# More sorted pairs, fewer own columns, and half of the sort comparisons on VectorE in a graph-network kernel

## The chip, the cores and the metric

The kernel runs on one core of one Trainium2 chip. A core has a matrix engine (TensorE, PE in the profile; its weight loads are listed as PEld), VectorE (DVE), ScalarE (ACT), GpSimd (POOL) and SyncE (SP), each with its own queue that is worked off in order, and 16 DMA engines. The metric is the time of one execution on the device, in microseconds. Before the change the median of 3 runs is 1998.59 us (1998.35 to 2001.69).

## What is computed

There are N = 6250 nodes with 128 features and E = 206250 edges with 128 features. Edge e belongs to the node `src[e]`. The edge features are summed by node, and a small network with a residual and a norm follows:

```python
edge_aggr = zeros((n, 128)).at[src].add(edge_features)
combined = concat([x, edge_aggr, global_expand], -1) @ W_c + b_c
h = softplus(combined @ W1 + b1)
h = softplus(h @ W2 + b2)
out = layernorm(x + h @ W3 + b3)
```

Nearly all of the time goes into the first line: 206250 rows of 512 bytes go to 6250 sums, in no useful order.

## The kernel before

Edges are handled in columns; a column is one edge on each partition. There are two kinds.

- **Own columns** hold 128 edges. PE spreads the node numbers over the columns of a square (two small bf16 products for each column, `name_own`, L810), DVE compares them with the node numbers (`equal_own`, L819), PE multiplies the rows by the result so that edges of one node in the column are added up (`sum_own`, L829), ACT copies the sums out of PSUM (`ready_own`, L840), DVE makes the row numbers (`number_own`, L847 and L849), and POOL issues one indirect DMA for each column that adds 128 rows to a table in DRAM (`totals_at`, L916). Three columns make a piece.
- **Pair columns** hold 105 edges each, and two make a pair. An edge has a slot by the bucket (256 nodes) of its node, so that a column comes out sorted by bucket. For a unit of three columns a 0/1 matrix is made (`compare`, L867 to L879): on DVE with one comparison (L869), or on ACT with three Abs (L876) and one Relu (L878). PE gathers the rows with it (`gather`, L887), ACT copies them out of PSUM in two halves (`settle`, L898), and POOL issues one indirect DMA for each pair (`place`, L932), which writes 128 pieces of two rows to their bucket in DRAM. Three pairs make a piece, and a piece has two units, one for each column of a pair.

Pair columns are written in nine groups, 0 to 8, and each is then reduced: a bucket's rows are loaded as chunks of 128 rows (`load`), DVE compares the row's code with 256 node numbers (`match`, L587), PE multiplies (L604, one product of two passes for each chunk; the profile counts two instructions) into PSUM, and DVE adds it to `sums_t` (L617). A group in `GROUPS` is (own columns, pairs, chunks of a full bucket, chunks of the last bucket). There are 25 buckets, so a group with (.., .., 11, 6) has 24 x 11 + 6 = 270 chunks whatever its columns.

Before a group's columns can be compared, the slots of its edges must be worked out (`positions`): sets of 20 columns go through some 7 steps that change between DVE (L372, L390 to L393, L402, L406, L423) and PE (L381, L397, L415, L417), and then through `pair_set`, `paired` and `pair_set2` (L511, L522, L529).

The order is written out by hand. `pieces` mixes the own and the pair pieces of a group evenly. `begins` gives each piece the time at which POOL would issue it, if POOL were never to wait: 1.3 us for a pair (`SCATTER`) and 1.87 us for an own column (`ADDED`). Every other step of a piece is given a time ahead of that: rows are loaded 34 us ahead, compared 17.5, gathered 14, settled 10.5. The reduce steps of group g - 1, the position steps of group g + 1 and the node steps are spread evenly over the stage of group g (L1117 to L1142). `SOONER = 5` puts the positions of both groups 6 and 7 into the stage of group 5, and those of group 8 into that of group 6. In the stage of group 8 the reduce of group 7 is spread up to 9 us after the last pair's time, and the reduce of group 8 after that. All steps are then sorted by time, and each engine's queue is filled in that order; nothing is tied to these times when the program runs.

Buffers that matter: 9 tiles of rows, 6 sets of sorted pairs, 8 tiles of chunks, 3 PSUM banks that gather, name and sum share, 2 PSUM banks for the sums of a reduce. All loads and stores go through SP's queue in the written order. After the last group come 19 more own columns (`LAST_OWN`), then `node_layers`: tables of the own columns are read back (`late`), joined, turned and added to `sums_t`, and the network follows for 13 tiles of up to 512 nodes.

Of the kernel before, what the change touches and what calls it, by code (L numbers as in the profile page):

```python
# [19 lines left out]
BL = 2 * P  # L20
EPS = 1e-5

GROUPS = ((18, 20, 2, 2), (14, 80, 7, 4), (22, 130, 11, 6), (31, 130, 11, 6), (31, 130, 11, 6),
          (31, 130, 11, 6), (31, 130, 11, 6), (66, 40, 4, 2), (20, 20, 2, 2))
LAST_OWN = 19
TAILS = ((1, 2), (2, 2), (4, 4), (4, 4))

# [29 lines left out]
NAMED, EQUALLED, SUMMED, READY, NUMBERED = 20.0, 17.5, 14.0, 10.5, 7.5  # L57
FIRST = 13.0
LEAD = 12
SHARES = {0: 2, 1: 2, 2: 2}  # L60
SHARE = 3
PREP, SUM, FILLED = 0.85, 0.97, 0.6
TOGETHER, BEHIND = 2, 4
NODES = (2, 6)
# [12 lines left out]
def kernel(  # L77
# [28 lines left out]
    NB = N // BL + 1  # L106
    TB = sum(g[1] for g in GROUPS)
    NC = 2 * TB
    KB = QUAD * (NB + 1)
    assert E >= PN * NC and all(2 * g[1] % STEP == 0 for g in GROUPS)  # L110
    assert NB * STEP <= 500 and KB <= P
# [6 lines left out]
    s0 = c0 = 0  # L118
    for n, (size, pairs, chunks, end) in enumerate(GROUPS):
        s1 = s0 + pairs  # L120
# [78 lines left out]
    with ExitStack() as phase:  # L199
# [661 lines left out]
        def compare(unit):  # L861
            i, lo, m, n = unit
            g, _, c, _, _ = pieces[i]
            slot = slot_of[g]
            hot = sort_p.tile([P, THREE, P], F32, name="sort_hot")
            hot_of[unit] = hot
            if (2 * i + n) % SHARES.get(g, SHARE) == 0:  # L867
                at = 2 * (c - groups[g][4] + lo) + n
                nc.vector.tensor_tensor(  # L869
                    hot[:PN, :m],  # L870
                    slot[:PN, at:at + 2 * m - 1:2].unsqueeze(2).to_broadcast([PN, m, P]),
                    slot_ps[:PN].unsqueeze(1).to_broadcast([PN, m, P]), op=ALU.is_equal)
                return
            for j in range(m):
                at = 2 * (c - groups[g][4] + lo + j) + n
                nc.scalar.activation(hot[:PN, j], by_slot[:PN], AF.Abs,  # L876
                                     bias=slot[:PN, at:at + 1], scale=-1.0)
            nc.scalar.activation(hot[:PN, :m], hot[:PN, :m], AF.Relu, bias=ones[:PN, :1],  # L878
                                 scale=-1.0)  # L879
# [130 lines left out]
        with tc.manual_schedule(engines={ET.PE, ET.DVE, ET.Activation, ET.SP}):  # L1010
# [66 lines left out]
            for i, t in enumerate(begins):  # L1077
                if t >= LOADED:
                    when(t - LOADED, lambda i=i: load_rows(i))
                if pieces[i][1] == "own":  # L1080
                    when(t - NAMED, lambda i=i: name_own(i))
                    when(t - EQUALLED, lambda i=i: equal_own(i))
                    when(t - SUMMED, lambda i=i: sum_own(i))
                    when(t - READY, lambda i=i: ready_own(i))
                    when(t - NUMBERED, lambda i=i: number_own(i))
                else:
                    when(t - CODED, lambda i=i: code_rows(i))
                mine = units(i)
                for u, unit in enumerate(mine):
                    late_by = SCATTER * pieces[i][3] * u / len(mine)  # L1090
                    when(t - COMPARED + late_by, lambda unit=unit: compare(unit))
                    when(t - GATHERED + late_by, lambda unit=unit: gather(unit))
                    when(t - SETTLED + late_by, lambda unit=unit: settle(unit))
                when(t, lambda i=i: scatter_rows(i))
# [332 lines left out]
```

## Time and profile before

| what | us |
|---|---|
| median of 3 runs | 1998.59 (1998.35 to 2001.69) |
| the profiled execution, whole | 2005.1 |
| its span, first to last instruction | 2002.9 |
| PE, DVE, ACT, POOL busy in the span | 1630.5, 1233.2, 1174.0, 1298.9 |
| granted PE clock over the span | 0.88 of full speed |
| stage of group 0 / 1 / 2 | 104 / 169 / 251 |
| stage of group 3 / 4 / 5 / 6 | 269 / 269 / 288 / 259 |
| stage of group 7 / 8 with the last own columns | 179 / 100 |
| after the last scatter | 115 |

A stage is the stretch from the first scatter of a group on POOL to that of the next group (0, 104, 273, 524, 793, 1062, 1350, 1609, 1788 and 1888 us from the start; the numbers come from counting POOL's scatters off against `pieces`). Groups 2 to 6 have the same 130 pairs each; group 2 reduces a small group (172 chunks), groups 3 to 7 each reduce 270.

How to read the rows: a row of groups gives line, engine, operation, tiles and shapes, count, then busy time, mean duration in ns, and the idle time just before, with what ended it. "issue" is time in which the profile sees nothing that the engine waits for. Row sums of PE overlap, since its products are pipelined; the union of PE's busy time in a stretch is in the table by stretches.

### The profile page before, as it was taken

The numbers are of one execution on the slowest core, as the hardware profiler recorded it, in microseconds if no ns is written. First come the engines' busy times: TensorE is split into PE (matmuls) and PEld (weight loads), VectorE is DVE, ScalarE is ACT, GpSimd is POOL, SyncE is SP. The second block draws the span as 40 slices with busy tenths as digits, with TensorE's granted clock in tenths as the row PEclk, the third lists the DMA queues.
The fourth block names the chain that finished last, engine by engine and source line by source line (L and its number), as shares of the span: only waits on it lengthen the run. The fifth ranks groups of instructions, "written<-read, shape, count | busy, mean of one in ns | idle before, by whom it ended". The sixth has DMA issues, their size and how long they took to land. (4 is left out here: it accounts for less than half of the span.)

```text
span 2002.9 us, 30974 instructions
## 1 busy us (share of the span) xinstructions
PE 1630.5 (81%) x10093; PEld 1395.4 (70%) x10093; DVE 1233.2 (62%) x2726; ACT 1174.0 (59%) x2921; POOL 1298.9 (65%) x1163
## 2 busy tenths in 40 slices
PE   5567777886889897998898888887888899969585
PEld 4456666775778776887676777766777788868464
DVE  7556645665556664676665776754555467756537
ACT  4255565666766666776677575666776654333045
POOL 2666565666666666666666665557666678778845
PEclk9577677888899989898998898899999899989888
DMA  9686465866777676876767666669777599966872
GB/s 338 164 253 184 140 194 163 236 190 178 214 210 202 196 204 192 237 215 181 209 183 237 190 191 174 185 168 265 207 213 214 156 249 227 229 148 164 211 207 66
DMA packets 401839, 399.72 MB, mean 200 GB/s; under 512 B 34286, under 2 KB 331323, under 8 KB 401673
## 3 DMA queue, kind: packets, MB, share of 16 engines
q1 hardware_dynamic: 322073, 275.77, 47.7%
q0 software_dynamic: 79600, 121.90, 23.5%
q8 instruction: 84, 1.38, 0.3%
q14 instruction: 82, 0.67, 0.1%
HBM read 245.79 MB, written 161.24 MB: 203 GB/s over the span
## 5 line engine op out<-in xcount | busy, mean ns | idle before, releaser
L932 POOL DMA_INDIRECT place<-pairs,pair x810 | 796.3, 983 | 420.9 <-issue 210.1
L604 PE MATMUL part<-hot,chunks 128*128 128x256 f32 x3440 | 928.8, 410 | 68.0 <-DVE hot L587 27.2
L898 ACT COPY pairs<-sorted 64x387 f32<-64x387 f32 (+2 forms) x1100 | 521.4, 474 | 588.3 <-PE sorted L887 213.1
L604 PEld LDWEIGHTS part<-hot,chunks 128*128 128x128 f32 x3440 | 663.2, 206 | 178.5 <-issue 59.7
L587 DVE SCALAR_TENSOR_TENSOR hot<-chunks,both_ps 128x512 f32<-128x512 f32 (+2 forms) x614 | 542.0, 896 | 221.8 <-PE part L604 105.4
L887 PE MATMUL sorted<-rows,sort_hot 105*128 105x129 f32 x3240 | 528.8, 307 | 90.0 <-ACT sort_hot L878 26.6
L887 PEld LDWEIGHTS sorted<-rows,sort_hot 105*128 105x128 f32 x3240 | 483.1, 216 | 156.4 <-issue 45.3
L916 POOL DMA_INDIRECT totals_at<-own_sum,own_at x283 | 440.4, 1556 | 227.7 <-issue 101.2
L876 ACT ACTIVATE sort_hot<-by_slot,slot 105x128 f32<-105x128 f32 x1006 | 331.7, 394 | 3.7
L878 ACT ACTIVATE sort_hot<-sort_hot,ones 105x384 f32<-105x384 f32 (+1 forms) x341 | 208.5, 611 | 11.1
L840 ACT COPY own_sum<-sorted 128x387 f32<-128x387 f32 (+3 forms) x99 | 46.3, 467 | 146.0 <-PE sorted L829 92.9
L869 DVE TENSOR_TENSOR sort_hot<-slot,both_ps 105x384 f32<-105x384 f32 (+1 forms) x209 | 112.5, 539 | 2.7 <-PE sorted L887 2.0
L819 DVE TENSOR_TENSOR same<-sorted,src_i 128x384 f32<-128x384 f32 (+3 forms) x99 | 53.0, 535 | 92.6 <-PE sorted L810 32.5
L423 DVE TENSOR_REDUCE slot<-small 105x20 f32<-105x500 f32 x81 | 54.8, 676 | 87.5 <-remote 29.4
L529 DVE TENSOR_SCALAR pair<-small,half_p 64x10 int32<-64x10 f32 x162 | 36.6, 226 | 114.2 <-remote 53.2
L829 PE MATMUL sorted<-own_rows,same 128*128 128x129 f32 x566 | 94.6, 303 | 9.1 <-issue 7.0
L829 PEld LDWEIGHTS sorted<-own_rows,same 128*128 128x128 f32 x566 | 85.1, 211 | 24.1 <-issue 17.9
L522 PEld LDWEIGHTS <-spread 104*128 104x128 bf16 x810 | 30.9, 100 | 69.7 <-DVE spread L511 39.7
L522 PE MATMUL small<-jump,spread 104*128 104x4 bf16 x810 | 33.7, 166 | 53.7 <-DVE spread L511 31.8
L617 DVE TENSOR_TENSOR sums_t<-sums_t,part 128x512 f32<-128x512 f32 (+1 forms) x104 | 68.3, 660 | 6.8 <-PE part L604 4.9
L417 PEld LDWEIGHTS <-ones_h 104*105 104x105 bf16 x405 | 37.5, 147 | 47.4 <-issue 40.8
L511 DVE TENSOR_TENSOR spread<-both_ps,starts 104x640 bf16<-104x640 f32 x81 | 66.8, 824 | 1.7
(179 smaller groups left out, 1081.6 us busy)
## 6 DMA issues: line engine op xcount, KB each, us to landing
rows<-in_edge_attr SPq DMA_DIRECT2D x266, 315.0 KB
chunks<-place SPq DMA_DIRECT2D x125, 408.0 KB
chunks<-place SPq DMA_DIRECT2D x120, 340.0 KB
own_rows<-in_edge_attr SPq DMA_DIRECT2D x91, 192.0 KB
chunks<-place SPq DMA_DIRECT2D x49, 272.0 KB
place<-pairs,pair POOLq DMA_INDIRECT x810
totals_at<-sums_t SPq DMA_DIRECT2D x3, 3072.0 KB
late<-totals_at SPq DMA_DIRECT2D x36, 256.0 KB
```

The lines of the kernel that those rows point to most:

```text
L511: nc.vector.tensor_tensor(past, twice_ps[:KB].unsqueeze(1).to_broadcast([KB, per_set, P]), own["starts"][:, q0:q0 + per_set].unsqueeze(2). ...
L587: nc.vector.scalar_tensor_tensor(hot[:, :e - a], chunks[i][:, a:e, D:W].to_broadcast([P, e - a, BL]), code_of(g), iota_ps.unsqueeze(1).to_ ...
L604: nc.tensor.matmul(part[:, b % 2, :], t[:, q, :D], hot[:, q - a], start=(lo + q == 0), stop=(last and q == hi - lo - 1))
L617: nc.vector.tensor_add(here, here, new)
L829: nc.tensor.matmul(out[:r, j, :], same[:r, j, :r], rows_at[i][:r, j, :], start=True, stop=True)
L869: nc.vector.tensor_tensor(hot[:PN, :m], slot[:PN, at:at + 2 * m - 1:2].unsqueeze(2).to_broadcast([PN, m, P]), slot_ps[:PN].unsqueeze(1).to ...
L876: nc.scalar.activation(hot[:PN, j], by_slot[:PN], AF.Abs, bias=slot[:PN, at:at + 1], scale=-1.0)
L878: nc.scalar.activation(hot[:PN, :m], hot[:PN, :m], AF.Relu, bias=ones[:PN, :1], scale=-1.0)
L887: nc.tensor.matmul(out[:, j, :], hot[:PN, j], rows_at[i][:PN, 2 * (lo + j) + n, :], start=True, stop=True)
L898: nc.scalar.copy(sets_at[i][64 * n:64 * n + 64, lo:lo + m, h, :W], out[64 * h:64 * h + 64, :m, :])
L916: s = nc.gpsimd.indirect_dma_start(out=copy_rows(copy, 0, N + 2), out_offset=bass.IndirectOffsetOnAxis(ap=at[:r, j:j + 1], axis=0), in_=ro ...
L932: s = nc.gpsimd.indirect_dma_start(out=dst, out_offset=bass.IndirectOffsetOnAxis(ap=at, axis=0), in_=rows[:, j].rearrange("p a b -> p (a b ...
```

## The change

The number of pairs goes from 810 to 850, and own columns from 283 to 217 (the total of edges is the same; 2 x 105 x 850 of them are in pairs). Own columns of the groups 0 to 8 go from 18, 14, 22, 31, 31, 31, 31, 66, 20 to 18, 0, 4, 25, 25, 25, 26, 44, 31; the 19 after the last group stay. Group 7 has 70 pairs instead of 40 and 172 chunks instead of 98; group 8 has 30 pairs instead of 20 and 74 chunks instead of 50. All chunks together go from 1720 to 1818. Of the units of three columns, every second is compared on DVE in all groups; before, that was so in the groups 0 to 2, and every third from group 3 on. In the two programs 288 comparisons stand on DVE instead of 209, and 288 on ACT (with their Abs) instead of 341.

```diff
-GROUPS = ((18, 20, 2, 2), (14, 80, 7, 4), (22, 130, 11, 6), (31, 130, 11, 6), (31, 130, 11, 6),
-          (31, 130, 11, 6), (31, 130, 11, 6), (66, 40, 4, 2), (20, 20, 2, 2))
+GROUPS = ((18, 20, 2, 2), (0, 80, 7, 4), (4, 130, 11, 6), (25, 130, 11, 6), (25, 130, 11, 6),
+          (25, 130, 11, 6), (26, 130, 11, 6), (44, 70, 7, 4), (31, 30, 3, 2))
...
-SHARES = {0: 2, 1: 2, 2: 2}
-SHARE = 3
+SHARE = 2
...
-            if (2 * i + n) % SHARES.get(g, SHARE) == 0:
+            if (2 * i + n) % SHARE == 0:
```

## The prediction

> **What bounds the kernel now.** I read the table by stretches first, cut at the stages of the groups, since the means of the page mix stages with different limits; then the waits of POOL in single stages; then the chain of waits near the end; then the rows of each operation that the change counts differently.
>
> ```profile
> core 0: us, PE busy (x) PEld busy (x) DVE busy (x) ACT busy (x) POOL busy (x), PEclk, DMA share, GB/s
> 104.00:273.00 169.00, 122.77 (x788) 105.57 (x788) 100.89 (x258) 100.03 (x249) 100.22 (x94) 0.73 0.62 181
> 273.00:524.00 251.00, 197.73 (x1262) 170.92 (x1262) 145.16 (x310) 158.96 (x397) 161.79 (x153) 0.84 0.67 195
> 524.00:793.00 269.00, 232.95 (x1495) 199.53 (x1496) 174.22 (x353) 183.71 (x464) 176.04 (x161) 0.92 0.74 209
> ...
> 1062.00:1350.00 288.00, 243.71 (x1602) 208.89 (x1600) 191.64 (x417) 184.12 (x465) 175.97 (x161) 0.92 0.68 191
> 1350.00:1609.00 259.00, 218.89 (x1240) 190.10 (x1240) 130.33 (x239) 178.87 (x453) 175.79 (x161) 0.91 0.74 208
> 1609.00:1788.00 179.00, 162.21 (x990) 145.13 (x989) 119.81 (x214) 76.23 (x192) 142.57 (x107) 0.96 0.85 212
> 1788.00:1888.00 100.00, 86.67 (x468) 73.23 (x468) 69.03 (x117) 22.33 (x55) 80.45 (x60) 0.93 0.77 181
> ```
>
> These are the groups 1, 2, 3, 5, 6, 7 and 8. PE is busy for 85 to 87% of the stages of groups 3 to 6, and for 91% of that of group 7. Is POOL the limit anywhere? Its timeline in group 3 and then in group 7:
>
> ```profile
> 651.32 0.97 POOL L932 DMA_INDIRECT place<-pairs,pair  x1 [0.30 <-issue]
> 654.70 0.97 POOL L932 DMA_INDIRECT place<-pairs,pair  x1 [2.41 <-DVE evens L393]
> 660.93 1.56 POOL L916 DMA_INDIRECT totals_at<-own_sum,own_at  x1 [2.70 <-ACT pairs L898]
> ...
> 1649.28 1.55 POOL L916 DMA_INDIRECT totals_at<-own_sum,own_at  x1 [0.30 <-issue]
> 1658.02 1.00 POOL L932 DMA_INDIRECT place<-pairs,pair  x1 [0.30 <-issue]
> ```
>
> With nothing to wait for, POOL takes 0.98 + 0.30 = 1.28 us for a pair and 1.56 + 0.30 = 1.86 us for an own column. Group 3 then needs 130 x 1.28 + 31 x 1.86 = 224 us of POOL and takes 269: POOL stands idle for the sort. Group 7 needs 40 x 1.28 + 66 x 1.86 = 174 and takes 179: POOL is the limit there. So it is in group 8: 64 us from its first scatter to its last pair, of which 20 x 1.28 + 20 x 1.86 = 62.8. The end hangs on that last pair:
>
> ```profile
> 1850.41 1.02 POOL place L932
> 1851.73 2.44 DMA place<-pairs,pair
> 1854.30 2.58 DMA chunks<-place
> ...
> 1857.19 0.70 DVE hot L587
> 1857.98 2.04 PE part L604 x4
> ```
>
> The last reduce starts at 1858.0, 70.1 us after the first scatter of group 8, and its last product ends at 1891.4; the loads for the layers stand behind its chunk loads on SP's queue. Durations for PE, dense and at full clock, from the chain in group 8:
>
> ```profile
> 1792.08 0.67 PE sorted L829 x6
> 1792.74 1.73 PE part L604 x8
> 1794.47 0.34 PE sorted L810 x6
> ...
> 1796.59 0.67 PE sorted L887 x6
> ```
>
> Eight instructions are four chunks, so a chunk costs 0.433 us; a pair (both columns) 2 x 0.67 / 3 = 0.447; an own column (0.67 + 0.34) / 3 = 0.34.
>
> **The change part by part.**
>
> *Own columns out of the groups 1 to 6:* 14, 18, 6, 6, 6 and 5, together 55. POOL waits for the sort there, so POOL's 1.86 us are the upper bound (102 us), reached only if the sort could go 17% faster by itself. The lower bound is PE's time alone at the stage's clock: 0.34 / 0.73 = 0.47 in group 1, 0.40 in group 2, 0.37 later, together 22 us. PE's idle time is likely to shrink in proportion, so I take PE's time times span by busy: 14 x 0.47 x 1.38 = 9, 18 x 0.40 x 1.27 = 9, 23 x 0.37 x 1.16 = 10: **-28 us**. I stay near the lower end since PE is the busiest engine there, and since in group 7, where own columns are most frequent, PE ran without a gap: an own column brought no stall of its own. DVE's 0.33 and ACT's 0.16 us for it lie beside that.
>
> *Position steps:* group 7 has 140 columns instead of 80, seven sets instead of four, and these stand in the stage of group 5 already beside the 13 sets of group 6; group 8 has three instead of two, in group 6. Group 5 with 17 sets took 19 us more than group 3 with 13, 4.75 a set; group 6 with 2 sets took 10 less than group 3, 0.9 a set. Four sets at 3 us: **+12** (4 to 19).
>
> *Comparisons:* some 14 units in each of the groups 3 to 6 go from ACT, 3 x 0.394 + 0.613 = 1.80 us, to DVE, 0.54. Who waits for ACT's matrices?
>
> ```profile
> PEld sorted L887 <- ACT sort_hot L878: 18.2, 6, 4.1
> PE sorted L887 <- ACT sort_hot L878: 15.2, 6, 3.5
> ```
>
> This is group 6, where DVE is busy for half of the time: I take two thirds of the 15.2, **-10**. In the groups 3 to 5 the same wait of PE is 1 to 2.5 us, and PE's waits for DVE's position steps are as long or longer (10.3 us for L393 in group 3 alone); DVE, 65% busy, gets 7.6 us more in each. I set both at nothing together: ACT's relief covers DVE's queue, and if it doesn't, each of these stages pays up to 7.6. Bounds for all four: -21 to +23.
>
> *Group 7:* POOL needs 44 x 1.86 + 70 x 1.28 = 171.4 instead of 174, **-3**. PE's busy 162 become 162 + 30 x 0.447 - 22 x 0.34 = 168, still under POOL, though only just; if PE needs the idle share of group 6 as well, this is +10.
>
> *Group 8 up to the last reduce:* POOL needs 31 x 1.86 + 30 x 1.28 = 96.1 instead of 62.8, +33.3. PE has 172 chunks of group 7 (74.5), 30 pairs (13.4) and 31 own columns (10.5), 98.4 in all, so the two limits meet: **+35**. The chunk loads wait for the pairs' DMA as before, 2.4 us.
>
> *The last reduce:* 74 chunks instead of 50. For two buckets PE now takes 8 products of 0.216 and a gap of 0.56, where it waits for DVE's comparison and sum; then 12 x 0.216 = 2.6 with the same gap. Twelve and a half times 0.87 less what overlaps at the ends: **+8** (6 to 10.4, the latter 24 x 0.433). The 19 own columns after the last pair, 19 x 1.86 = 35 us, end before that reduce does, and the loads that follow it on SP keep their place: nothing. More bytes for chunks (98 x 70 KB, 6.8 MB) at a DMA share of 0.77 are hidden by loads that are five ahead.
>
> Sum: -28 + 12 - 10 - 3 + 35 + 8 = **+14 us**. The profiled execution took 2005.1 (span 2002.9), 6.5 over the median of 1998.6; on the median that is **2012.6**.
>
> *A rule beside a row.* DVE's extra comparisons could cost POOL directly. The row: a pair's POOL instruction takes 981 ns in group 2, where half of the comparisons are on DVE, and 981 in group 3, with a third. So they cost POOL nothing here, and the sum has nothing for it. [...]
>
> **The rivals.**
>
> *A. The sort speeds up with POOL's work taken out: faster.* Groups 2 and 3 take 44 and 45 us more than POOL's need (251 against 207, 269 against 224) though PE does 35 us less in group 2. That speaks for a pace set by the written order rather than by PE's work, so that an own column taken out is worth near its 1.86 us. The place is groups 1 and 2: PE's granted clock is 0.73 and 0.84 there against 0.92. If fewer gaps bring both to 0.92, PE's busy time alone falls by 122.8 x (1 - 0.73 / 0.92) + 197.7 x (1 - 0.84 / 0.92) = 25 + 17 = 42 us. In place of my -28 the own columns then give -28 - 42 = -70, and the time is 2012.6 - 42 = **1970.6**. It decides once an own column is worth over 0.51 + 14 / 55 = 0.76 us. Against it: group 7's dense PE. (The Trainium skill, "TensorE: Matmul & The Clock Gate", Part 1, has the clock at half after an idle window of about 3.4 us and at full after a busy one; this trace grants 0.5 or 1.0 in stretches of 3.4 us and more, so the mean follows gaps. Whether they go with the own columns no row shows.)
>
> *B. The terms cancel:* own columns at 0.76 us, within 0.2% of **1998.6**. What the middle gains, the end gives back.
>
> *C. DVE becomes the limit of the groups 3 to 5* through the comparisons and the sets: +7.6 in each and 4.75 a set, 23 + 7 more, **2042**. For it: PE waits for DVE in group 5 for some 30 us already, with DVE at 67%. Against: ACT's relief.
>
> **How the numbers follow.** My forecast 0.47, A 0.35, B 0.10, C 0.08. The measurement tells 0.2%, 4 us, from no change. Faster 0.36 (A and a corner of the forecast), same 0.11, slower 0.53. The range for 8 in 10 goes from A with a slightly dearer own column, 1962, to the forecast with the upper ends of the sets (+7), group 7 (+13) and the last reduce (+2), 2034. The likeliest case by itself: 2003 to 2034.
>
> **What would show it.** In the profile after: groups 1 and 2 shorter by about 10 us each (A: by 25 and more, and a granted clock near 0.9); groups 3 and 4 within 5 us of before; group 5 longer by some 6; group 6 shorter by 12, and PE's wait for L878's matrices (L877 there) a third; POOL without waits in groups 7 and 8, and 96 to 100 us from group 8's first scatter to its last pair instead of 64; 41 us for the last reduce. Wrong it is if the first seven stages together shrink by over 50 us, or if group 8 grows by less than 25.

## The result and the profile after

The changed kernel takes 1964.07 us (median of 4 runs, 1960.85 to 1968.49) against 1998.47 for the kernel before (4 runs, 1988.35 to 2001.69). The ratio is 0.9839, with a 95% interval of 0.9809 to 0.987: 1.6% faster, where 0.7% slower was forecast. The time lies in the range, 6.5 us from rival A's.

The profiled execution took 1960.85 us (span 1959.0), 44 less than the profiled one of before. The table by stretches, cut at the first scatter of each group, shows where they went. After the stretch and its length come busy time and count of PE, PE's weight loads, DVE, ACT and POOL, then the granted clock of PE, the DMA share and GB/s. Changed kernel, groups 1, 2, 3, 5, 6, 7 and 8:

```profile
core 0: us, PE busy (x) PEld busy (x) DVE busy (x) ACT busy (x) POOL busy (x), PEclk, DMA share, GB/s
101.70:251.50 149.80, 112.88 (x717) 96.62 (x716) 95.31 (x240) 95.33 (x239) 77.91 (x80) 0.72 0.61 190
251.50:481.10 229.60, 185.87 (x1196) 162.32 (x1196) 140.07 (x294) 157.68 (x396) 133.08 (x135) 0.87 0.68 202
481.10:736.10 255.00, 224.96 (x1465) 191.78 (x1464) 177.50 (x360) 160.89 (x403) 166.08 (x155) 0.95 0.77 217
...
990.90:1273.40 282.50, 238.82 (x1627) 207.29 (x1626) 208.50 (x458) 161.15 (x403) 166.18 (x155) 0.92 0.68 192
1273.40:1526.90 253.50, 214.35 (x1251) 188.74 (x1250) 137.15 (x254) 160.49 (x402) 167.50 (x156) 0.92 0.75 210
1526.90:1703.70 176.80, 168.79 (x1001) 148.61 (x1000) 116.13 (x195) 89.17 (x225) 137.56 (x114) 0.99 0.89 233
1703.70:1798.20 94.50, 91.39 (x557) 82.05 (x556) 70.32 (x113) 37.84 (x94) 76.52 (x60) 1.00 0.93 236
```

The last row ends with the last pair of group 8. The stages of the two profiled executions, cut in the same way to a tenth, with POOL's need (1.28 us for each pair, 1.86 for each own column of the group) beside them:

| stage | before | after | change | forecast | POOL's need before, after |
|---|---|---|---|---|---|
| 0 | 104.2 | 101.7 | -2.5 | 0 | |
| 1 | 169.1 | 149.8 | -19.3 | -9 | 128.4, 102.4 |
| 2 | 252.3 | 229.6 | -22.7 | -9 | 207.3, 173.8 |
| 3 | 267.4 | 255.0 | -12.4 | -2.5 | 224.1, 212.9 |
| 4 | 269.8 | 254.8 | -15.0 | -2.5 | 224.1, 212.9 |
| 5 | 289.0 | 282.5 | -6.5 | +6 | 224.1, 212.9 |
| 6 | 259.1 | 253.5 | -5.6 | -12 | 224.1, 214.8 |
| 7 | 176.9 | 176.8 | -0.1 | -3 | 174.0, 171.4 |
| 8, up to the last pair | 64.9 | 94.5 | +29.6 | | |
| own columns after it | 35.2 | 39.7 | +4.5 | | |
| after the last scatter | 114.9 | 121.0 | +6.1 | | |
| the last three | 215.0 | 255.2 | +40.2 | +43 | |

The forecast for single stages is the prediction's own list of signs; its -12 for group 6 leaves out the one set that comes to that stage. Cut to a tenth, group 7 of the kernel before takes 176.9 us and not 179.

The end of the program grew as forecast. The stages 0 to 6 shrank by 84 us, where the terms for them (-28, +12, -10) gave 26, and where over 50 was the prediction's sign of being wrong. So the question is the middle: what is an own column worth there?

### The profile page after: what moved, and what is told of

It reads as the page before. It is cut to its first block, busy times and chain, and to the rows that moved or that the text cites. A ratio compares the mean times of both kernels' runs of the same rounds, so it can differ in the third digit from the quotient of the medians.

```text
span 1959.0 us, 31386 instructions
## 1 busy us (share of the span) xinstructions
PE 1636.9 (84%) x10273; PEld 1409.6 (72%) x10273; DVE 1285.5 (66%) x2791; ACT 1113.7 (57%) x2755; POOL 1232.1 (63%) x1137
## 4 chain that ended last, share of the span: by engine, by line
PE 45%; DVE 7%; ACT 4%; issue 4%; another core or an unknown queue 3%; DMA 3%; POOL 2%; SPq 0%; ACTq 0%; DVEq 0%; POOLq 0%
PE part L603 26%; PE sorted L886 11%; ACT pairs L897 2%; DVE hot L586 2%; PE sorted L828 2%; PE late_ps L1295 1%; POOL place L931 1%; DMA zx_sb<-z_x 1%; DMA totals_at<-own_sum,own_at 1%; ACT sort_hot L875 1%; POOL totals_at L915 1%; DVE spread L510 1%; PE sorted L809 1%; PE small L521 1%
## 5 line engine op out<-in xcount | busy, mean ns | idle before, releaser
L931 POOL DMA_INDIRECT place<-pairs,pair x850 | 832.0, 979 | 494.3 <-issue 215.7
L603 PE MATMUL part<-hot,chunks 128*128 128x256 f32 x3636 | 953.3, 403 | 44.7 <-DVE sums_t L618 17.4
L897 ACT COPY pairs<-sorted 64x387 f32<-64x387 f32 (+2 forms) x1152 | 545.3, 473 | 641.6 <-PE sorted L886 253.2
L586 DVE SCALAR_TENSOR_TENSOR hot<-chunks,both_ps 128x768 f32<-128x768 f32 (+2 forms) x638 | 572.4, 908 | 168.2 <-PE part L603 83.1
L915 POOL DMA_INDIRECT totals_at<-own_sum,own_at x217 | 338.2, 1559 | 170.9 <-issue 86.8
L875 ACT ACTIVATE sort_hot<-by_slot,slot 105x128 f32<-105x128 f32 x850 | 279.4, 391 | 4.2
L877 ACT ACTIVATE sort_hot<-sort_hot,ones 105x384 f32<-105x384 f32 (+1 forms) x288 | 175.6, 610 | 9.3
L868 DVE TENSOR_TENSOR sort_hot<-slot,both_ps 105x384 f32<-105x384 f32 (+1 forms) x288 | 155.4, 540 | 4.4 <-PE sorted L886 4.3
L616 DVE TENSOR_TENSOR sums_t<-sums_t,part 128x512 f32<-128x512 f32 (+1 forms) x104 | 68.6, 660 | 20.9 <-PE part L603 12.4
L510 DVE TENSOR_TENSOR spread<-both_ps,starts 104x640 bf16<-104x640 f32 x85 | 70.1, 824 | 2.0
L828 PE MATMUL sorted<-own_rows,same 128*128 128x129 f32 x434 | 67.8, 293 | 3.1 <-ACT pairs L897 3.0
L828 PEld LDWEIGHTS sorted<-own_rows,same 128*128 128x128 f32 x434 | 63.2, 205 | 8.2 <-ACT pairs L897 4.3
```

Of the source, the lines that this page charges most:

```text
L510: nc.vector.tensor_tensor(past, twice_ps[:KB].unsqueeze(1).to_broadcast([KB, per_set, P]), own["starts"][:, q0:q0 + per_set].unsqueeze(2). ...
L586: nc.vector.scalar_tensor_tensor(hot[:, :e - a], chunks[i][:, a:e, D:W].to_broadcast([P, e - a, BL]), code_of(g), iota_ps.unsqueeze(1).to_ ...
L603: nc.tensor.matmul(part[:, b % 2, :], t[:, q, :D], hot[:, q - a], start=(lo + q == 0), stop=(last and q == hi - lo - 1))
L828: nc.tensor.matmul(out[:r, j, :], same[:r, j, :r], rows_at[i][:r, j, :], start=True, stop=True)
L868: nc.vector.tensor_tensor(hot[:PN, :m], slot[:PN, at:at + 2 * m - 1:2].unsqueeze(2).to_broadcast([PN, m, P]), slot_ps[:PN].unsqueeze(1).to ...
L875: nc.scalar.activation(hot[:PN, j], by_slot[:PN], AF.Abs, bias=slot[:PN, at:at + 1], scale=-1.0)
```

## The experiments

All of these runs fell on other chips of the same kind, on which the kernel before takes 1738 to 1744 us instead of 1998; each time below stands beside that of the kernel before on the same chip. Where stages of "the kernel before" on such a chip are meant, they are those of two kernels that are like it in the groups concerned (only the planned times, or only the comparisons, differ, experiments 4 and 5) and that take the same time within 0.3%: 138, 208, 225, 225, 225 and 225 us for the groups 1 to 6. Experiments 1 to 4 and 7 are single runs, and the kernel before spreads over 9 to 14 us on such a chip, so what they say is read from the stages.

**1. Thirty-two own columns moved to the end.** All 14 of group 1 and 18 of the 22 of group 2 go behind the last group; nothing else changes.

```diff
-GROUPS = ((18, 20, 2, 2), (14, 80, 7, 4), (22, 130, 11, 6), (31, 130, 11, 6), (31, 130, 11, 6),
+GROUPS = ((18, 20, 2, 2), (0, 80, 7, 4), (4, 130, 11, 6), (31, 130, 11, 6), (31, 130, 11, 6),
...
-LAST_OWN = 19
+LAST_OWN = 51
```

> The kernel before, with the own columns of the groups 1 and 2 alone taken out (0 and 4 instead of 14 and 22); they come after the last group (51 instead of 19), so the time as a whole says nothing, only the stages do. PE-time theory (the prediction's): the stages of groups 1 and 2 shrink by 9 us each, 169 to 160 and 252 to 243. Price theory (an own column costs some 1.3 us in these stages, whatever the reason): 169 to 150 and 252 to 229, as in the changed kernel. The stages 3 to 6 stay within 4 us of before by both, which also tells how well a stage repeats.

It took 1756.86 us against 1743.48. The stages of the groups 1, 2 and 3 in the table by stretches:

```profile
102.10:231.70 129.60, 101.19 (x675) 87.09 (x676) 90.56 (x228) 85.41 (x215) 77.86 (x80) 0.76 0.71 220
231.70:405.90 174.20, 165.71 (x1216) 149.07 (x1216) 142.14 (x295) 162.85 (x409) 133.04 (x134) 0.96 0.89 268
405.90:630.60 224.70, 211.39 (x1505) 189.91 (x1503) 174.20 (x353) 187.10 (x477) 175.59 (x161) 0.98 0.89 249
```

Group 2 takes 174.2 us, where POOL needs 130 x 1.28 + 4 x 1.86 = 173.8. It lost 208 - 174.2 = 33.8 us for 18 columns, 1.88 each: POOL's full time for an own column. In group 1 the 14 columns gave 138 - 129.6 = 8.4, 0.6 each; there POOL needs only 102 of the 130 us. (That stage without own columns varies from 125 to 131 us in the runs below, so 0.5 to 0.9 each is as close as it gets.) Group 3 kept its columns and stands at its need of 224.1. The whole program is slower, since at the end the 32 columns cost 55 us, 1.7 each.

**2. POOL's add taken away, the rest of the own column kept.** Here the 160 own columns of the groups 1 to 6 of the kernel before are loaded, named, summed and copied, but not added to the table, so these edges are missing in the sums.

```diff
                 at, rows = own_of.pop(i)
+                if 0 < g < 7:
+                    return
```

> The kernel before without POOL's indirect adds of the own columns in the groups 1 to 6; all of PE's, DVE's and ACT's work for them stays (left out: 160 of the 283 adds to the table). POOL theory (an own column's price is POOL's 1.86 us after all): group 3 shorter by some 30 to 45 us, group 2 by 20 to 30, group 1 by 15. PE-time and handoff theories: POOL stands idle for the sort in these stages anyway, so each stage stays within 6 us.

It took 1657.85 us against 1743.48. Groups 3 and 5:

```profile
409.90:622.70 212.80, 208.47 (x1492) 187.24 (x1492) 172.70 (x350) 182.01 (x462) 126.68 (x130) 0.99 0.85 252
836.20:1061.40 225.20, 217.29 (x1594) 194.01 (x1592) 192.25 (x420) 183.67 (x465) 126.75 (x131) 0.98 0.79 237
```

PE's work is the same, and 86 us are gone: POOL's adds were the price. The adds' DMA transfers went with them, so this run alone does not tell POOL's instruction from its transfers; that a stage stands at POOL's need, with no wait between its instructions over the usual 0.3 us (the waits are shown below), does. The rows also show the next limit, and why it is 86 us and not 160 x 1.86 = 298. POOL would need 166 us in group 3, but PE is busy for 208.5 of 212.8 at a clock of 0.99. In group 5, with its 17 position sets, the stage stays at 225 with and without POOL's adds.

**3. The opposite: POOL's add kept, the rest taken away.** The own columns of the groups 1 to 6 of the kernel before lose their name and sum on PE, their comparison on DVE and their place in the PSUM banks; rows are loaded, copied by ACT and added by POOL as they are, to row numbers that are spread by the partition and not by the node. (The run is called "gap kept"; the kernel is the one before, not the changed one.)

```diff
         def name_own(i):
+            if bare(i):
+                return
...
+            if bare(i):
+                summed[i] = rows_at[i]
+                return
             same = equal.pop(i)
```

> The kernel before, whose own columns in the groups 1 to 6 keep their place, their rows' load, their copy on ACT and their add on POOL, but lose PE's name and sum and DVE's comparison and the PSUM banks for these (left out: the sum of edges of one node in a column; each add goes to rows 0, 48, 96 and so on). POOL theory: groups 3 to 6 stay at 224 us. PE and handoff theories: group 3 shorter by 31 x 0.37 = 11 us or more, group 2 by 9 or more.

It took 1744.22 us against 1738.42, and the groups 2 to 6 took 207.6, 224.9, 224.7, 224.5 and 224.5 us. PE's share of an own column, the very thing that the prediction had charged, costs nothing in these stages. (Group 1 took 142.0 against 138; why was not tried.)

**4. The written order.** Rival A also said that the pace might come from the order of the queues. In the kernel before, own columns of the groups 1 to 6 are planned at 0.7 us instead of 1.87, so that everything else is written nearer together.

```diff
-                now += (SCATTER if kind == "pair" else ADDED) * k
+                now += (SCATTER if kind == "pair" else PLANNED if 0 < g_of < 7 else ADDED) * k
```

> The kernel before with all its work, but in the written order an own column of the groups 1 to 6 counts 0.7 us instead of 1.87, so that the steps of the pair pieces on both sides of an own piece move together. Written-order theory (stages follow the planned time; 31 own columns plan for 58 us of group 3): group 3's planned time falls from 227 to 191 us, and its stage by some 20 to 40 us from 267; group 2's by 15 to 30. Work theory (PE time or handoffs, which all stay): the stages stay within 6 us.

1742.03 us against 1743.48, and no stage of the groups 1 to 6 differs by over a microsecond from that of the first kernel of experiment 5, which has the planned times of before. The planned time of an own column sets nothing here.

**5. The comparisons.** First alone in the kernel before, then taken back in the changed kernel.

```diff
-SHARES = {0: 2, 1: 2, 2: 2}
-SHARE = 3
+SHARES = {}
+SHARE = 2
```

> The kernel before, with every second unit compared on DVE in all groups. The prediction: groups 3 to 5 unchanged, group 6 shorter by 10 us, 1988 in all. Rival, that the comparisons are what made the groups 3 and 4 faster (own columns at 1.3 us explain 8 of the 12 to 15 us by which each shrank): groups 3 and 4 shorter by 5 to 7 us each, 1975 to 1985 in all. Second rival, DVE is the limit in groups 3 to 5: each longer by up to 7.6, about 2010.

1746.41 us against 1743.48, ratio 1.0028 with an interval of 1.0008 to 1.0049. Group 6 took 224.6, as without.

```diff
-SHARE = 2
+SHARES = {0: 2, 1: 2, 2: 2}
+SHARE = 3
...
-            if (2 * i + n) % SHARE == 0:
+            if (2 * i + n) % SHARES.get(g, SHARE) == 0:
```

> The changed kernel with the comparisons as before (every third unit on DVE from group 3 on). If the placement of the comparisons is worth nothing, as in the kernel before on this chip (ratio 1.003), this is within 0.5% of the changed kernel. If ACT, with 25 us more work in each of the groups 3 to 6, holds up PE's gathers now that POOL leaves the sort less slack, groups 3, 4 and 6 are longer by 5 to 12 us each and the whole by 15 to 40.

1706.79 us, against 1708.17 for the changed kernel and 1738.42 for the one before on that chip; the ratios to before, 0.9811 (0.9771 to 0.9851) and 0.9822 (0.9781 to 0.9862), can't be told apart. The gain that was forecast for group 6 is not there.

**6. The changed kernel on such a chip.**

> The changed kernel once more, now beside the kernel before on the chip of the experiments, where the kernel before took 1743 us and the stages of its groups 3 to 6 stood at POOL's need (130 x 1.28 + 31 x 1.86 = 224 us). POOL theory: the price of an own column there is POOL's 1.86 us until PE (about 211 us busy in group 3) becomes the limit: group 2 from 208 to 176, groups 3 and 4 from 225 to 214, group 5 (PE 215, seven sets more) 220 to 226, group 6 from 225 to 215, the end +40 as on the first chip; together about 1695, 3% faster. PE-time theory of the prediction: groups 2 to 6 shorter by 2 to 9 each, the end +40, together about 1755, slower.

1708.17 us, a ratio of 0.9822, which agrees with the 0.9839 of the first chip. Groups 3, 5, 6 and 8 up to the last pair:

```profile
402.50:616.70 214.20, 204.45 (x1457) 184.45 (x1458) 176.07 (x357) 158.37 (x395) 166.02 (x155) 0.98 0.90 257
...
830.10:1061.20 231.10, 217.08 (x1604) 192.52 (x1604) 204.23 (x450) 157.13 (x392) 166.05 (x155) 0.98 0.82 234
1061.20:1276.40 215.20, 196.13 (x1266) 178.27 (x1264) 139.02 (x258) 166.37 (x418) 167.60 (x157) 0.96 0.87 247
...
1448.70:1543.20 94.50, 88.51 (x523) 79.49 (x524) 68.34 (x109) 33.95 (x85) 76.50 (x60) 0.95 0.92 233
```

Groups 3 and 6 stand at POOL's need, 212.9 and 214.8. Of the groups 2 to 6, group 5 alone does not: 231 against 212.9. Is that the position sets?

**7. The own columns alone.** The kernel before with all 55 own columns taken out of the groups 1 to 6, and put at the end.

```diff
-GROUPS = ((18, 20, 2, 2), (14, 80, 7, 4), (22, 130, 11, 6), (31, 130, 11, 6), (31, 130, 11, 6),
-          (31, 130, 11, 6), (31, 130, 11, 6), (66, 40, 4, 2), (20, 20, 2, 2))
-LAST_OWN = 19
+GROUPS = ((18, 20, 2, 2), (0, 80, 7, 4), (4, 130, 11, 6), (25, 130, 11, 6), (25, 130, 11, 6),
+          (25, 130, 11, 6), (26, 130, 11, 6), (66, 40, 4, 2), (20, 20, 2, 2))
+LAST_OWN = 74
```

> The kernel before with one part of the change alone: the 55 own columns taken out of the groups 1 to 6 (0, 4, 25, 25, 25 and 26 stay), and put behind the last pair instead (74 there, not 19); pairs, chunks, position sets and the placement of the comparisons as before. Theory 1 (an own column costs POOL's 1.86 us in the groups 1 to 6 wherever the sort keeps up): group 1 -9, group 2 -33, groups 3, 4 and 6 -11, -11 and -10, group 5 between -5 and -11; some 80 us in all, and the 55 at the end cost up to 1.86 each, 102, of which the 32 moved in an earlier run gave 55; the time is about 15 to 20 us above the kernel before. Theory of the prediction (0.5 us each): -28 in the middle and some 98 at the end, 70 us slower. On a chip that runs the kernel before in some 2000 us, the stages of groups 1 to 6 should shrink as they did with the whole change there, by 19, 23, 12 and 15 in groups 1 to 4, if the own columns alone made it; where group 3 and 4 shrink by less than 8, the comparisons had a part in it.

1762.75 us against 1740.6. Groups 3, 5 and 6:

```profile
405.70:619.10 213.40, 206.41 (x1469) 185.47 (x1467) 169.78 (x342) 186.09 (x473) 166.14 (x156) 0.98 0.90 259
832.40:1052.70 220.30, 212.15 (x1546) 189.18 (x1545) 191.00 (x416) 172.00 (x435) 166.18 (x156) 0.98 0.88 245
1052.70:1267.80 215.10, 195.18 (x1244) 177.10 (x1242) 127.40 (x230) 188.08 (x478) 167.54 (x157) 0.96 0.87 246
```

With 127.6 and 174.3 for the groups 1 and 2 and 213.3 for group 4 the six stages are 1164.0 instead of 1245.5: 81.5 us for 55 columns, 1.48 each. Group 5 with 17 sets takes 220.3; with the 20 sets of the changed kernel it took 231, and 228.5 with the comparisons of before. So three more sets cost 8 us there, or 11 together with the comparisons on DVE, and the one more in group 6 cost nothing, since that stage stays at POOL's need.

**8. The position sets moved.** In the changed kernel, group 7's seven sets go from the stage of group 5 to that of group 6.

```diff
-SOONER = 5
+SOONER = 6
```

> The changed kernel with the position sets of group 7 (seven of them, and the row codes) planned in the stage of group 6 and no longer in that of group 5, which then has the 13 sets of group 6 alone; group 8's three sets stay in the stage of group 6, which then has ten. The changed kernel again took 1708 us on another chip, with 231.2 us for group 5's stage against 212.9 that POOL needs there, and 215.1 for group 6's against 214.8. Theory 1 (the twenty sets, PE and DVE work, are what holds group 5 above POOL's need): group 5 goes to 214 to 217, group 6 stays at 215 to 219 since groups 3 and 4 carry 13 sets at POOL's need; 12 to 16 us less in all, about 1694. Theory 2 (group 5 is held by something else, or a set costs 0.9 us wherever it stands): group 5 loses 6 us at most, group 6 gains as much, no change beyond 3 us. Theory 3 (the predicted upper price, 4.75 a set): group 5 loses 18, group 6 gains 33, slower by 15.

1694.07 us against 1740.6 for the kernel before, a ratio of 0.9728 (0.9699 to 0.9758). Groups 5 and 6:

```profile
831.90:1045.30 213.40, 207.19 (x1471) 186.69 (x1469) 176.67 (x359) 159.34 (x398) 166.15 (x155) 0.98 0.90 256
1045.30:1260.40 215.10, 199.92 (x1398) 182.23 (x1398) 165.98 (x351) 164.00 (x412) 167.52 (x156) 0.97 0.86 245
```

Group 5 falls from 231 to POOL's need. Group 6 takes seven more sets, 27 us more of DVE and 4 more of PE, and stays where it was: POOL covers them.

**9. A smaller group 7,** without and with the moved sets.

```diff
-          (25, 130, 11, 6), (26, 130, 11, 6), (44, 70, 7, 4), (31, 30, 3, 2))
+          (25, 130, 11, 6), (26, 130, 11, 6), (44, 70, 6, 3), (31, 30, 3, 2))
```

> The changed kernel with 6 and 3 chunks in group 7 instead of 7 and 4 (its fullest bucket has 720 of then 768 rows). 25 chunks less, 25 x 0.433 = 10.8 us of PE. If PE is the limit from group 8's first scatter to the last reduce (in the changed kernel it is busy for 97% of that stretch and for 99% with its weight loads), the whole is shorter by 8 to 11 us. If POOL is (96.1 us needed of the 94.5 from group 8's first scatter to the last pair's end), by 0 to 4.

1701.01 us, ratio to before 0.9781 (0.9742 to 0.9821). The stretch from the first scatter of group 8 to its last pair stayed at 94.5, though its reduce is 25 chunks shorter: POOL sets it. The 7 us came behind it: the reduce of group 7 ends at 1547.8 instead of 1556.2, and the last reduce at 1590.1 instead of 1596.8.

> The same move of the sets, and group 7 with six chunks a bucket and three over instead of seven and four, 25 chunks less. The latter alone took 1701 us on another chip where the changed kernel took 1708. If the two gains are in different stages they add: 13 and 7 less than the changed kernel, about 1687, and the end of the last pair to the last own column stays at 38.6. If group 7's lists being complete later holds something, the 7 are lost.

1684.53 us, 0.9671 (0.9643 to 0.97): the two gains add.

**10. Own columns put back where they are cheap.** If a column costs 0.6 us in group 1 and 1.86 elsewhere, group 1 is the place for it. On top of 9, group 1 gets its 14 columns again, out of the groups 3 to 8.

```diff
-GROUPS = ((18, 20, 2, 2), (0, 80, 7, 4), (4, 130, 11, 6), (25, 130, 11, 6), (25, 130, 11, 6),
-          (25, 130, 11, 6), (26, 130, 11, 6), (44, 70, 6, 3), (31, 30, 3, 2))
+GROUPS = ((18, 20, 2, 2), (14, 80, 7, 4), (4, 130, 11, 6), (23, 130, 11, 6), (23, 130, 11, 6),
+          (23, 130, 11, 6), (23, 130, 11, 6), (42, 70, 6, 3), (28, 30, 3, 2))
```

> The changed kernel with the moved sets and the smaller group 7 (that took 1684.5 us), and 14 own columns put back into group 1, where the first experiments priced one at 0.6 us only (138.5 against 129.6 us for 14), out of the groups 3 to 6 (23 each instead of 25, 25, 25, 26), 7 (42 instead of 44) and 8 (28 instead of 31), where POOL's 1.86 us is the price as long as PE keeps up. If PE keeps up everywhere: group 1 +8.5, groups 3 to 5 -3.7 each, 6 -5.6, 7 -3.7, 8 -5.6; 17 us less, 1667. If PE is the next limit (it is busy for 207 of 213 us in groups 4 and 5, 166 of 172 in group 7, and without POOL's adds the kernel before took 212.8 to 213.5 for groups 3 and 4): those stages stay above 211 and 170, half of the 26 is lost, and the time is 1680 to 1684. If an own column in group 1 costs 1.86 like elsewhere: no change, 1684.

1671.84 us against 1744.23, a ratio of 0.961 (0.9563 to 0.9657), the fastest of all. Groups 1, 3 and 6:

```profile
101.70:241.20 139.50, 107.60 (x749) 93.81 (x749) 97.97 (x251) 93.42 (x235) 100.04 (x95) 0.79 0.76 222
...
415.00:625.10 210.10, 204.69 (x1453) 185.17 (x1454) 175.18 (x353) 155.37 (x389) 162.80 (x154) 0.98 0.91 258
...
1046.40:1256.60 210.20, 200.43 (x1393) 181.84 (x1391) 165.26 (x350) 162.36 (x407) 162.89 (x154) 0.98 0.86 249
```

Group 1 paid 10 us for 14 columns, 0.7 each. Groups 3 to 6 need 130 x 1.28 + 23 x 1.86 = 209.2 of POOL and take 210.1 to 211.0; PE is busy for 205 of them in groups 3 and 5, so little more is to be had from POOL in groups 3 to 5.

## Why the prediction was wrong

**The step that failed** is the first term, own columns out of the groups 1 to 6 at 28 us, 0.5 each, and in it the sentence that POOL waits for the sort there, from which it followed that PE's time is the price. The runs on the other chips show 81.5 us for the 55 columns in its place, 1.48 each, and POOL's whole 1.86 us in the groups 2 to 4 and 6 (experiments 1 and 7). I took POOL's idle time of 45 us in group 3 for a sort that can't keep up. Here are the waits of POOL in that stage of the kernel before, on the first chip (what waited and for what, us in total, times, longest):

```profile
POOL place L932 <- issue: 33.6, 107, 1.0
POOL place L932 <- ACT pairs L898: 18.9, 9, 3.9
POOL totals_at L916 <- ACT pairs L898: 9.0, 3, 4.0
POOL totals_at L916 <- issue: 8.6, 24, 1.6
```

131 of POOL's 161 instructions waited for no other engine, nearly all of them only the 0.3 us that lies between any two, and the excess sits in some 20 long waits. It is tempting to read from this that POOL was the pace and something else halted it now and then. But the waits don't tell. Pairs come three to a piece, so most go out back to back in any case, and in group 3 of experiment 2, where POOL would need 166 of the 212.8 us and PE is busy for 208.5, so that POOL is starved by the sort, its waits look the same:

```profile
POOL place L934 <- ACT pairs L898: 50.4, 19, 5.4
POOL place L934 <- issue: 25.6, 84, 0.3
POOL place L934 <- ACT rows L792: 6.1, 11, 1.6
```

Where POOL is the pace, it looks otherwise. On one of the other chips POOL's waits in group 3 of the kernel before, with half of the comparisons on DVE, are:

```profile
POOL place L932 <- issue: 30.2, 99, 0.3
POOL totals_at L916 <- issue: 7.3, 24, 0.3
POOL place L932 <- DMA place<-pairs,pair: 2.7, 9, 0.3
```

No wait is longer than 0.3, and the stage is POOL's need to within a microsecond. Experiments 1, 2, 3 and 7 show the price on these chips from both sides.

On the first chip the six stages shrank by the same 81.5 us (1506.7 to 1425.2), with the position sets inside. That the two sums are alike is chance: on the chip of experiment 6 the whole change took 72 us out of them (1245.5 to 1173.5), and there group 2 gave 33.5, not 22.7. The time over POOL's need was 275 us before and 296 after; in the groups 3, 4 and 6 it is 43, 46 and 35 before, and 42, 42 and 39 after. Much of it is halts of ACT, DVE and PE, which only this chip shows (last section). That the stages there are POOL's need and a rest that doesn't depend on the own columns fits these two traces, but is not shown: PE's 233 busy us and some 38 of halts would fill the 267 of group 3 as well, and no experiment was made on that chip.

**Rival A** had the sign and nearly the time, and it was right that a column is worth near POOL's 1.86 us, but neither of its reasons held, so that its time came within 6.5 us is luck. The planned time sets no pace (experiment 4). The clock of group 1 did not rise (0.73 to 0.72), that of group 2 only to 0.87; those of groups 3 and 4 rose from 0.92 and 0.91 to 0.95. Where it could be tried, the columns were worth more because POOL's own time was the price. Rival B's 0.76 us a column is out by the same 1.48. Rival C's costs, of the sets and of the comparisons on DVE, show in group 5 alone, 11 of its 30 us; whether DVE or PE is the limit there was not tried.

**Position sets:** +12 was forecast for four; on the other chips three in group 5 cost 8 to 11 and the one in group 6 nothing. The size held by luck, since the rule of so much for each set did not: experiment 8 shows ten sets in group 6 for nothing. A set costs only once PE and DVE run past POOL's need.

**Comparisons:** -10 was forecast and nothing came. In the changed kernel PE's waits in group 6 are these:

```profile
PE sorted L886 <- issue: 10.8, 8, 3.9
PE sorted L886 <- DVE same L818: 9.7, 3, 5.1
PE sorted L886 <- ACT pairs L897: 9.0, 4, 4.5
```

The wait for ACT's matrices, 15.2 us before, is down to 1.2, where a third was forecast. Others have taken its place, as they must where PE does not set the length of the stage: its idle time is the rest, whatever its label. The stage's -5.6 is less than the 9.3 that POOL saves there for five columns.

**Group 7:** -3 forecast, -0.1 measured on the first chip and -3 on the others (175.2 to 172.3). PE is busy for 168.8 of the 176.8 us on the first, as forecast (168), and POOL needs 171.4; which of the two kept the 3 us there was not tried.

**Group 8 up to the last reduce:** +35 forecast, and +36.2 measured: the reduce starts 106.3 us after the first scatter (1810.0 - 1703.7), instead of 70.1. The two limits came out nearly alike, as forecast: the stretch to the last pair is 94.5 us, of which PE is busy for 91.4, and POOL needs 94.2 for it, since one of the 31 own columns comes behind the last pair. The chain of waits of the changed kernel runs along POOL up to the last reduce (start, us, what):

```profile
1798.53 1.56 POOL totals_at L915
...
1805.98 3.00 DMA totals_at<-own_sum,own_at
1808.97 0.95 DVE hot L586
...
1809.96 5.46 PE part L603 x24
```

But what released a wait is inferred by the profile, and experiment 9 says otherwise for the time behind the last pair. With 25 chunks less in the reduce of group 7 the last reduce starts 100.4 us after the group's first scatter, instead of 108.9 on that chip, with the stretch to the last pair unchanged. So behind the last pair it was PE, still at the reduce of group 7, that held up the last reduce.

**The last reduce:** 41 us forecast, 39.2 measured (1810.0 to 1849.2), +5.8 instead of +8.

**DVE's comparisons and POOL.** The page after has 288 comparisons on DVE instead of 209, and POOL's pair:

```profile
L931 POOL DMA_INDIRECT place<-pairs,pair x850 | 832.0, 979 | 494.3 <-issue 215.7
```

979 ns instead of 983: no price, as the row of before had said. The Trainium skill, "SBUF — State Buffer", "Who interferes with whom", says that a VectorE instruction with at most one SBUF input, outside the two-port modes, does not contend with GpSimd. The comparison reads one operand from SBUF and one from PSUM, and this trace agrees.

**The clock.** Group 2 ran at 0.97 with 9 us of PE idle (experiment 7: 174.3 less 165.1) and at 0.84 with 53 us of it (the kernel before, first chip). The rule of the Trainium skill, "TensorE: Matmul & The Clock Gate", Part 1, by which the clock falls after an idle window and rises after a busy one, fits these two. No run here shows the clock as a cause of its own.

## What to carry to other kernels

An engine's idle time does not tell whether work taken from it is worth nothing or its full duration, and neither does the spread of its waits: they look alike where the engine is starved and where something halts its producers. Two runs told it here, one without the engine's part of a step and one without all the other parts (experiments 2 and 3), and so did a trace of a chip without such halts, where the stage is as long as POOL's need and none of its waits is longer than 0.3 us. The price of one and the same step differs by stage (0.6 to 0.7 us in group 1, 1.86 in group 2), so compare each stage with the need of each engine and move work to stages where the limiting engine has room, as experiments 8 and 10 do. An idle engine's waits for one producer are no gain by themselves: when that producer is made faster, the same idle time gets another label.

## What was not expected of the hardware

The same program takes 1998 us on one chip and 1738 to 1744 on four others. Between the trace of the kernel before on the first chip and that of experiment 4, which has the same work, lie 263 us, and 261 of them in the groups 1 to 6 (1506.7 against 1245.5); group 7 takes 176.9 and 175.5. Most of this goes with halts on the first chip: ACT waits 39 times and DVE 43 times for something that the profile calls "remote", 119 and 158 us in all. With overlapping ones counted once, such waits of ACT, DVE and PE cover 205 us of the groups 1 to 6 before and 175 after; none comes behind group 6, and no trace from the other chips has one. Here is one, in the timeline of the kernel before on that chip (start, us, engine, line, what, and in brackets the idle time before it and what ended it):

```profile
573.33 0.98 POOL L932 DMA_INDIRECT place<-pairs,pair  x1 [0.30 <-issue]
...
574.61 0.98 POOL L932 DMA_INDIRECT place<-pairs,pair  x1 [0.30 <-issue]
576.57 0.97 ACT L898 COPY pairs<-sorted 64x387 f32<-64x387 f32 x2 [4.03 <-remote]
577.34 0.68 DVE L423 TENSOR_REDUCE slot<-small 105x20 f32<-105x500 f32 x1 [7.87 <-remote]
...
577.81 0.97 POOL L932 DMA_INDIRECT place<-pairs,pair  x1 [2.23 <-ACT pairs L898]
...
578.83 0.17 PE L397 MATMUL small<-evens,lower_h 104*104 104x5 bf16 x1 [3.95 <-DVE evens L393]
```

ACT and DVE stand for 4 and 8 us, POOL goes on until it has nothing left, and PE is the last to start again. What released ACT and DVE the profile can't name ("remote"); DVE's input from PE had been made at 571.1. The cause stays open, since no experiment ran on that chip. For the change it mattered little: the ratios there and elsewhere, 0.9839 and 0.9822, have intervals that overlap.
